# Scaling the second choice's rows on ScalarE and adding them on TensorE in the last turn from rows to columns

## The chip, the cores and the metric

The kernel runs on one core of one Trainium2 chip, as one program with one launch. The metric is the device time in microseconds (us) from start to end of an execution; smaller is better. Three runs of the kernel before gave a median of 8828.61 us (8826.25 to 8833.44).

## The reference

The model takes an image batch of 2 x 256 x 56 x 56 in f32 and applies four layers: a windowed attention, a positional embedding, six Mamba layers followed by a feed-forward over the better half of the tokens, and at last an attention over the two images and a mixture of 8 experts with two choices for each token. Only the end of the last layer is touched here:

```python
rw, re = jax.lax.top_k(probs, TOP_K)          # TOP_K = 2
rw = rw / jnp.maximum(rw.sum(-1, keepdims=True), 1e-12)
combine = jnp.zeros((N, E), tokens.dtype).at[jnp.arange(N)[:, None], re].set(rw)
out = tokens
for e in range(E):
    h = jax.nn.gelu(tokens @ w1[e] + b1[e], approximate=False)
    y = h @ w2[e] + b2[e]
    out = out + combine[:, e:e + 1] * y
...
x = _from_tokens(t, x)     # tokens x channels back to channels x tokens
```

So each token gets its own row plus two expert rows, each times a factor of its own, and the result is then turned from rows (a token in a partition) to columns (a channel in a partition) and written out.

## The kernel before

The span has three parts. The convolution part and the long Mamba part take it up to about 7900 us; neither is touched. The rest is the function `tail_phase`, in which the tokens lie as rows: each image (batch index `b`, 0 or 1) has 3136 tokens in 28 tiles of 112, and four tiles make a group, so that an image has seven groups, called g0 to g6 below.

The order of the instructions on every engine in that part is made by a small planner, the class `Flow` (L1199). Every piece of work is a Python generator. It yields `("take", name)` for a buffer of a ring, `need(flag)` for a condition, and an engine's name with a cost in us; the planner keeps one clock for each engine, resumes the generator that is due first, and what a generator issues at that moment is appended to the engines' queues. The costs thus decide the order, not the chip. On the chip each engine then runs its queue strictly in order and waits on semaphores. SP (SyncE) issues the plain DMAs, also strictly in order; POOL issues the gathers and scatters by index.

The mixture of experts runs in this order. Rows are gathered by expert (L1396, `pair<-m_d`), turned by TensorE into PSUM (L2005), copied by VectorE (L1340, `hid`), multiplied (L2030), copied back (L1340, `pair`), turned again (L2045), put through the Gelu by ScalarE (L2053, `deep`), multiplied again (L2030), copied by ScalarE (L1338, `out`) and scattered by POOL to a table `r2_d` in DRAM (L1986), whose first half holds every token's row from its first choice and whose second half that from its second choice. One such pass handles two blocks of 128 rows, and an image has 28 of them. PSUM tiles come from rings: three called `turn`, three called `mid`, two called `sum`.

`combine(b, g)` (L2069) closes a group. It adds the experts' biases to the tokens `t` (L2089), waits until all experts of that image are done, and then does for `c` = 0 and 1 (first and second choice): take one of the six buffers `rows`, load 112 x 4 x 256 values from `r2_d` into it (L2099, 448 KB), and add four tiles of it, each times its column of `gates`, to `t` by VectorE with `add_times` (L1388), after which the buffer is given back. Then `turn` transposes `t` group-wise into two `turn` tiles, one for each half of the 256 channels (L1348, four transposes to a tile), ScalarE copies both to a `chan` tile (L1338), and SP writes that to the output (L2114).

```python
def turn(dst, src, n, engines=("ACT", "DVE")):
    for k in range(2):
        ps = yield take("turn")
        for i in range(n):
            nc.tensor.transpose(ps[:, chunk(i, TK)], src(i)[:, chunk(k, P)], ident[:TK, :TK])
        yield "PE", 0.2 * n
        yield move(engines[k], dst[:, k, : n * TK], ps[:, : n * TK])
        flow.give("turn", ps)
```

The groups of image 0 are combined while the experts of image 1 run (about 8605 to 8750 us). The groups of image 1 come when no other work is left (8797 us to the end): fourteen loads, fifty-six adds, fifty-six transposes, fourteen copies, seven writes. In SP's queue the fourteen loads of image 1 stand one behind the other, first choices of g0 to g6, then second choices of g0 to g6, and the seven writes behind them. With six buffers, the first six loads start at once and the seventh to the fourteenth each wait for an add that gives a buffer back.

Of the kernel before, what the change touches and what calls it, by code (L numbers as in the profile page):

```python
# [15 lines left out]
AF = mybir.ActivationFunctionType  # L16
# [5 lines left out]
P = 128  # L22
# [23 lines left out]
TK = 112  # L46
# [4 lines left out]
GT = 4 * TK  # L51
# [8 lines left out]
def chunk(c, n=NT):  # L60
    return slice(c * n, (c + 1) * n)
# [1198 lines left out]
def tail_phase(ctx: ExitStack, tc: tile.TileContext, I, t2_d, out, rest):  # L1260
# [6 lines left out]
    nc = tc.nc  # L1267
# [7 lines left out]
    flow = Flow()  # L1275

    def fixed(shape, name, dtype=F32):
        return cp.tile(shape, dtype, name=name)
# [19 lines left out]
    def take(name):  # L1298
        return "take", name

    def need(*flag):
        return "need", flag

    ident = fixed([P, P], "tl_ident")
# [18 lines left out]
    t, mv, rs, up, off, score = [], [], [], [], [], []  # L1323
# [12 lines left out]
    def move(which, dst, src):  # L1336
        if which == "ACT":
            nc.scalar.copy(dst, src)  # L1338
        else:
            nc.vector.tensor_copy(dst, src)  # L1340
        return which, 0.65
# [10 lines that stand above are left out]
# [35 lines left out]
    def add_times(b, i, src, factor):  # L1387
        nc.vector.scalar_tensor_tensor(  # L1388
            t[b][:, i, :], src, factor, t[b][:, i, :], ALU.mult, ALU.add
        )  # L1390
# [105 lines left out]
    def per_batch(shape, name, dtype=F32):  # L1496
        return [fixed(shape, f"{name}_{b}", dtype) for b in range(B)]
# [4 lines left out]
    gates = per_batch([TK, 2, NTK], "gates")  # L1502
# [566 lines left out]
    def combine(b, g):  # L2069

        yield need("weighed", b)
        yield need("expert", b, 3 * g + 2)
        comb = yield take("comb")
        ps = yield take("mid")
        for n in range(4):
            nc.tensor.transpose(ps[:NE, chunk(n, TK)], lg[b][:, 4 * g + n, :], ident[:TK, :TK])
        yield "PE", 0.4
        yield move("ACT", comb, ps[:NE, :GT])
        flow.give("mid", ps)
        for n in range(0, 4, 2):  # L2080
            ps = yield take("mid")
            for i in range(2):
                nc.tensor.matmul(
                    ps[:TK, chunk(i, C)], lhsT=comb[:, chunk(n + i, TK)], rhs=mb2,
                    start=True, stop=True,
                )
            yield "PE", 0.9
            own = t[b][:, 4 * g + n : 4 * g + n + 2, :].rearrange("p n c -> p (n c)")
            nc.vector.tensor_tensor(own, own, ps[:TK], ALU.add)  # L2089
            yield "DVE", 0.7  # L2090
            flow.give("mid", ps)
        flow.give("comb", comb)
        for n in range(NQ // 2):
            yield need("expert", b, n)
        if b == 0:
            yield need("loaded_expert", 1, 3 * g + 1)
        for c in range(2):
            z = yield take("rows")
            nc.sync.dma_start(  # L2099
                z[:TK],  # L2100
                r2_d[b][c * S + g * GT : c * S + (g + 1) * GT, :].rearrange(
                    "(n p) c -> p n c", p=TK
                ),
            )
            yield "SP", 1.3
            yield "wait", 2.0
            for n in range(4):
                i = 4 * g + n
                add_times(b, i, z[:TK, n, :], gates[b][:, c, i : i + 1])
            yield "DVE", 2.0  # L2110
            flow.give("rows", z)
        o = yield take("chan")
        yield from turn(o, lambda i: t[b][:, 4 * g + i, :], 4, ("ACT", "ACT"))
        nc.sync.dma_start(out_v[b, :, :, chunk(g, GT)], o)  # L2114
        yield "wait", 3.0
        flow.give("chan", o)
# [54 lines left out]
    for b in range(B):  # L2171
        flow.start(*[back(b, g) for g in range(NG)])
        flow.start(*[combine(b, g) for g in range(NG)])
# [130 lines left out]
```

## Time and profile before

| what | value |
|---|---|
| runs: median (lowest to highest) | 8828.61 us (8826.25 to 8833.44) |
| profiled execution, its own time | 8834.56 us |
| its span, first to last instruction | 8832.8 us, mean granted TensorE clock 0.97 |
| PE / DVE / ACT / POOL busy over the span | 84% / 89% / 75% / 86% |
| a load of `rows` in the last stretch | 448 KB, 7.8 to 9.7 us from issue to landing |
| an add to `t` (L1388, 112x256) | 477 ns |
| a copy of a turned tile by ScalarE / by VectorE (128x448) | 532 ns / 615 ns |
| a transpose of 112x112 in the tail (L1348) | 257 ns at full clock, up to 450 ns |

Busy shares over the whole span are those of the Mamba part and say little about the tail; rows of single stretches have to be read. `busy` counts the time in which an engine works on an instruction; a DMA share near or above 1 means that all 16 DMA engines of the core are at work all the time. The granted clock is the share of full speed at which TensorE was let run. In the tail one column of the 40 slices is 221 us, so the last stretch of 35 us must be asked for by a window of its own.

### The profile page before, as it was taken

What the parts mean: (1) busy time and instruction counts of PE and PEld (TensorE: products, weight loads), DVE (VectorE), ACT (ScalarE), POOL (GpSimd) and SP (SyncE); (2) the same over time, 40 slices, a digit from 0 to 9 for tenths busy, and PEclk for the clock granted to TensorE, in tenths of its full rate; (3) what the DMA queues carried; (4) which work ended last, traced back from release to release, by engine and by line L of the source; (5) the groups of instructions that cost most, each with busy time, mean ns of one, the idle gap of its engine ahead of it and who ended that gap; (6) DMA issues with size and microseconds to landing.
All of it is one profiled execution on the core that took longest, in us unless ns stands there. A gap on an engine that the chain in (4) does not pass through costs nothing.

```text
span 8832.8 us, 106454 instructions
## 1 busy us (share of the span) xinstructions
PE 7458.7 (84%) x32350; PEld 3282.6 (37%) x32350; DVE 7845.9 (89%) x7140; ACT 6659.6 (75%) x15914; POOL 7609.8 (86%) x5255
## 2 busy tenths in 40 slices
PE   9988888888888888888888888888888888867987
PEld 6553333333333333333333333333333333325776
DVE  3339999999999999999999999999999999985664
ACT  1238888888888888888888888888888888863432
POOL 2339999999999999999999999999999999982354
PEclk9999999999999999999999999999999999988988
DMA  2335565655656555556566565556556565543225
GB/s 85 100 116 127 135 135 126 136 131 132 135 132 133 131 132 135 134 133 148 136 137 137 127 133 134 130 133 135 130 133 134 127 138 130 134 118 93 65 72 150
DMA packets 698246, 1118.31 MB, mean 127 GB/s; under 512 B 80060, under 2 KB 675843, under 8 KB 697667
## 3 DMA queue, kind: packets, MB, share of 16 engines
q1 hardware_dynamic: 682888, 1072.49, 52.5%
q0 software_dynamic: 14784, 39.01, 1.5%
q8 instruction: 257, 4.21, 0.2%
q14 instruction: 317, 2.60, 0.1%
HBM read 892.62 MB, written 218.60 MB: 126 GB/s over the span
## 4 chain that ended last, share of the span: by engine, by line
PE 44%; ACT 33%; DVE 13%; issue 6%; DMA 2%; POOL 2%; SPq 0%; ACTq 0%; DVEq 0%; POOLq 0%
ACT da L896 12%; PE mm L683 9%; PE mm L665 8%; PE mm L821 6%; DVE da L934 4%; PE acc L949 4%; DVE x L934 4%; ACT dt L742 2%; DVE x L926 2%; ACT dt L750 2%; ACT hz L695 2%; PE mm L754 2%; ACT dt L749 2%; ACT hz L700 2%; ACT dt L758 1%
## 5 line engine op out<-in xcount | busy, mean ns | idle before, releaser
L913 POOL TENSOR_TENSOR x<-dtur,bc 128x900 f32<-128x900 f32 x2688 | 4717.0, 1793 | 7.8 <-DMA dtur<-dtu_d 7.6
L896 ACT ACTIVATE da<-dtr,am 128x451 f32<-128x451 f32 x5376 | 3417.0, 641 | 323.7 <-DVE x L934 153.9
L934 DVE TENSOR_TENSOR_SCAN da<-da,x 128x902 f32<-128x902 f32 x1512 | 3040.1, 2031 | 97.5 <-ACT da L896 70.9
L934 DVE TENSOR_TENSOR_SCAN x<-da,x 128x902 f32<-128x902 f32 x1176 | 2341.5, 2018 | 46.6 <-ACT da L896 38.2
L926 POOL TENSOR_TENSOR x<-x,bc 128x896 f32<-128x896 f32 x1176 | 2080.1, 1784 | 80.9 <-DVE x L934 80.9
L926 DVE TENSOR_TENSOR x<-da,bc 128x896 f32<-128x896 f32 x1512 | 1604.1, 1075 | 20.5 <-ACT state L922 9.0
L949 PE MATMUL acc<-x,sum_w 128*32 128x448 f32 x10752 | 1382.5, 568 | 59.2 <-DVE x L926 33.9
L683 PE MATMUL mm<-u,w_cv 128*128 128x448 f32 x2656 | 1093.8, 554 | 67.0 <-ACT tail L678 56.9
L665 PE MATMUL mm<-xn,w_z 128*128 128x448 f32 x1328 | 587.0, 564 | 196.5 <-ACT dt L758 116.7
L683 PEld LDWEIGHTS mm<-u,w_cv 128*128 128x128 f32 x2656 | 478.6, 190 | 677.7 <-issue 375.9
L665 PE MATMUL mm<-xn,w_u 128*128 128x448 f32 x1328 | 579.0, 558 | 121.2 <-ACT hz L695 111.8
L821 PE MATMUL mm<-hz,w_out 128*128 128x448 f32 x1344 | 553.7, 555 | 107.9 <-ACT tail L678 56.3
L949 PEld LDWEIGHTS acc<-x,sum_w 128*32 128x32 f32 x10752 | 266.2, 111 | 966.7 <-issue 732.7
L754 PE MATMUL mm<-dt,mb_ident 128*128 128x448 f32 x666 | 342.1, 595 | 257.6 <-ACT state L922 139.4
L737 PE MATMUL mm<-xd,w_dt 128*128 128x448 f32 x664 | 339.2, 592 | 217.2 <-ACT dtu L745 128.6
L912 ACT COPY x<-state 128x2 f32<-128x2 f32 x2688 | 437.1, 187 | 0.1
L665 PEld LDWEIGHTS mm<-xn,w_z 128*128 128x128 f32 x1328 | 225.4, 189 | 564.5 <-ACT dt L758 236.4
L665 PEld LDWEIGHTS mm<-xn,w_u 128*128 128x128 f32 x1328 | 231.5, 189 | 457.8 <-ACT hz L695 223.1
L821 PEld LDWEIGHTS mm<-hz,w_out 128*128 128x128 f32 x1344 | 243.3, 191 | 417.9 <-issue 189.2
L766 POOL TENSOR_TENSOR dtu<-dt,hz 128x448 f32<-128x448 f32 x336 | 330.9, 985 | 76.6 <-PE mm L755 76.6
L695 ACT ACTIVATE hz<-mm,vec 128x448 f32<-128x448 f32 x332 | 209.2, 630 | 243.1 <-PE mm L683 238.8
L944 PE MATMUL acc<-hz,w_sk 128*128 128x448 f32 x672 | 347.0, 600 | 31.7 <-DVE hz L963 31.7
(377 smaller groups left out, 9536.9 us busy)
## 6 DMA issues: line engine op xcount, KB each, us to landing
dtr<-dt_d SPq DMA_DIRECT2D x1344, 224.0 KB, 4.4
dtur<-dtu_d SPq DMA_DIRECT2D x1344, 224.0 KB, 6.7
bc<-bc_d SPq DMA_DIRECT2D x336, 448.0 KB, 7.8
dt_d<-dt SPq DMA_DIRECT2D x336, 224.0 KB, 6.2
dtu_d<-dtu SPq DMA_DIRECT2D x336, 224.0 KB, 2.0
rows<-r_d SPq DMA_DIRECT2D x28, 448.0 KB, 7.9
xg<-in_x SPq DMA_DIRECT2D x26, 448.0 KB, 8.9
bm<-in_edge SPq DMA_DIRECT2D x16, 539.0 KB, 4.6
```

Of the source, the lines that this page charges most:

```text
L665: nc.tensor.matmul(ps, lhsT=w[:, k, chunk(d, P)], rhs=Q["xn"][:, k, :], start=(k == 0), stop=(k == 1),)
L683: nc.tensor.matmul(ps, lhsT=w_cv[:, 4 * d + k, :], rhs=M["u", d][:, k : k + T], start=(k == 0), stop=(k == 3),)
L695: nc.scalar.activation(hz(j)[:, d, :], M["mm"], AF.Identity, bias=layer_of(j + 1)["cb"][:, d : d + 1])
L754: nc.tensor.matmul(ps, lhsT=ident, rhs=M["dt"][:, d, :], start=True, stop=False)
L821: nc.tensor.matmul(ps, lhsT=layer_of(j - 1)["w_out"][:, d, chunk(k, P)], rhs=gated(j - 1)[:, d, :], start=(d == 0), stop=False,)
L896: nc.scalar.activation(D[i][:, chunk(g, R)], dtr[:, 2 * pr + g, :], AF.Exp, scale=L["am"][:, col : col + 1],)
L912: nc.scalar.copy(x[:, :, 0:1], states(i))
L913: nc.gpsimd.tensor_tensor(x[:, :, 1:], Q[k][1][:, 2 * pr : 2 * pr + 2, :], wide(Q["bc"][:, ng, :]), ALU.mult)
L926: engine.tensor_tensor(both(X[i])[:, :, 1 : T + 1], both(h)[:, :, 1 : T + 1], wide(QS[j]["bc"][:, 4 + ng, :T]), ALU.mult,)
L934: nc.vector.tensor_tensor_scan(h, D[i], X[i], 0.0, ALU.mult, ALU.add)
L944: nc.tensor.matmul(acc[0][:, :T], lhsT=L["w_sk"][:, k, :], rhs=Q["hz"][:, k, :], start=True, stop=False,)
L949: nc.tensor.matmul(acc[0][chunk(g, HD), :T], lhsT=sum_w, rhs=both(X[i - 1 + g // 2])[:, g % 2, 1 : T + 1], start=False, stop=(ng == 3), ti ...
```

## The change

For image 1 and the second choice (`b and c`), the four tiles of the loaded buffer are no longer added to `t` by VectorE: ScalarE multiplies each in place with its factor (an activation Copy with a scale from `gates`). The buffer is kept. Then the turn of image 1 is written out: for each half of the channels and each of the four tiles, two matmuls with the identity as the moving operand accumulate in the same PSUM place, one with the tile of `t` and one with the scaled tile as the stationary operand, in place of one transpose. The first half is copied to `chan` by VectorE, the second by ScalarE (both by ScalarE before). The buffer is given back only after both halves are turned and copied.

For image 0 the instructions stay the same, but the planner's cost of the four adds is 1.7 in place of 2.0, for image 1's first choices too.

```diff
             for n in range(4):
                 i = 4 * g + n
-                add_times(b, i, z[:TK, n, :], gates[b][:, c, i : i + 1])
-            yield "DVE", 2.0
+                factor = gates[b][:, c, i : i + 1]
+                if b and c:
+                    nc.scalar.activation(z[:TK, n, :], z[:TK, n, :], AF.Copy, scale=factor)
+                else:
+                    add_times(b, i, z[:TK, n, :], factor)
+            if b and c:
+                yield "ACT", 2.2
+            else:
+                yield "DVE", 1.7
+                flow.give("rows", z)
+        o = yield take("chan")
+        if b == 0:
+            yield from turn(o, lambda i: t[b][:, 4 * g + i, :], 4, ("ACT", "ACT"))
+        for k in range(2 * b):
+            ps = yield take("turn")
+            for n in range(4):
+                for x, last in ((t[b][:, 4 * g + n, :], False), (z[:TK, n, :], True)):
+                    nc.tensor.matmul(
+                        ps[:, chunk(n, TK)], lhsT=x[:, chunk(k, P)], rhs=ident[:TK, :TK],
+                        start=not last, stop=last,
+                    )
+            yield "PE", 1.6
+            yield move(("DVE", "ACT")[k], o[:, k, :], ps[:, :GT])
+            flow.give("turn", ps)
+        if b:
             flow.give("rows", z)
-        o = yield take("chan")
-        yield from turn(o, lambda i: t[b][:, 4 * g + i, :], 4, ("ACT", "ACT"))
         nc.sync.dma_start(out_v[b, :, :, chunk(g, GT)], o)
```

The planner's order on the engines for image 1 becomes: on ScalarE the 24 scalings of g0 to g5, then the copies of the second halves of g0 to g3, then the four scalings of g6, then the copies of g4 to g6; on SP the first thirteen loads, the write of g0, the fourteenth load (second choice of g6), then the writes of g1 to g6; on TensorE the turns of g0 to g3 interleaved, of which the second half of g3 needs a PSUM tile that ScalarE's copy of g0 frees. The fourteenth load goes into the buffer that held g0's second choice. For image 0 the order of SP shifts: before, its fourteen loads stand between the writes in runs of 4, 3, 1, 2, 3, 1; after, in runs of 4, 1, 1, 3, 1, 2, 2. The order of the expert passes' pieces among these shifts too.

## The prediction

> **What bounds the kernel now.** I read the page for the span first; its slices are 221 us wide, so the tail is asked for by windows, by the order of time in the last 45 us, and by the waits of the engines and of SP's queue. The page begins:
>
> ```profile
> span 8832.8 us, 106454 instructions
> ## 1 busy us (share of the span) xinstructions
> PE 7458.7 (84%) x32350; PEld 3282.6 (37%) x32350; DVE 7845.9 (89%) x7140; ACT 6659.6 (75%) x15914; POOL 7609.8 (86%) x5255
> ```
>
> These shares belong to the Mamba part, which the change doesn't touch. The order of time of the last stretch (start, length, engine, line, what, count, idle before):
>
> ```profile
> 8795.28 0.99 POOL L1986 DMA_INDIRECT r_d<-out,goal  x1 [0.30 <-issue]
> 8797.76 17.67 SPq L2099 DMA_DIRECT2D rows<-r_d  x14
> 8801.51 3.30 DVE L1388 SCALAR_TENSOR_TENSOR t<-rows,gates,t 112x256 f32<-112x256 f32 x8 [11.63 <-DMA rows<-r_d]
> 8805.09 19.85 DVE L1388 SCALAR_TENSOR_TENSOR t<-rows,gates,t 112x256 f32<-112x256 f32 x48 [0.28 <-DMA rows<-r_d]
> ...
> 8816.94 11.45 SPq L2114 DMA_DIRECT2D out<-chan  x7
> ...
> 8824.77 2.60 PE L1348 MATMUL turn<-tl_ident,t 112*128 112x112 f32 x16 [1.69 <-ACT chan L1338]
> 8826.35 1.64 ACT L1338 COPY chan<-turn 128x448 f32<-128x448 f32 x3 [0.34 <-DMA out<-chan]
> ```
>
> After the last scatter SP issues fourteen loads. VectorE adds from 8801.5 to 8824.9 almost without a break, which looks like a VectorE bound. The windows say that it is not alone (length; busy of PE, PEld, DVE, ACT, POOL; clock, DMA share, GB/s):
>
> ```profile
> 8808.00:8812.00 4.00, 0.00 (x0) 0.00 (x0) 4.00 (x10) 0.00 (x0) 0.00 (x0) 0.50 1.11 276
> 8814.00:8816.00 2.00, 2.00 (x8) 1.36 (x9) 2.00 (x6) 0.36 (x1) 0.00 (x0) 0.50 1.12 279
> 8820.00:8822.00 2.00, 2.00 (x10) 1.55 (x10) 2.00 (x6) 1.24 (x3) 0.00 (x0) 0.50 1.12 282
> 8822.00:8824.00 2.00, 1.07 (x9) 0.86 (x8) 2.00 (x6) 0.00 (x0) 0.00 (x0) 0.93 1.04 384
> 8826.00:8828.00 2.00, 1.37 (x8) 1.02 (x6) 0.00 (x0) 1.52 (x4) 0.00 (x0) 0.50 0.95 360
> 8828.00:8833.00 5.00, 0.00 (x0) 0.00 (x0) 0.00 (x0) 0.00 (x0) 0.00 (x0) 0.50 0.61 225
> ```
>
> The DMA engines are full from 8800 to 8828. Fourteen loads of 458,752 B at 279 GB/s are 23.0 us, seven writes at about 370 GB/s are 8.7 us: 31.7 us of the 35.0 from the first load's issue to the end. A group's four adds take 1.65 us (3.30 for two) and a load's transfer takes 1.64: two equal bounds side by side.
>
> Ahead of that, the experts of image 1 run beside image 0's combine (windows, then who waited for whom from 8600 to 8797, us in total, times, longest):
>
> ```profile
> 8610.00:8620.00 10.00, 3.97 (x19) 3.13 (x18) 2.96 (x6) 1.69 (x5) 7.86 (x8) 0.87 1.02 266
> 8640.00:8650.00 10.00, 6.13 (x30) 4.41 (x28) 3.87 (x8) 2.15 (x6) 7.78 (x8) 0.91 0.82 219
> 8710.00:8720.00 10.00, 7.49 (x30) 5.33 (x29) 3.67 (x8) 1.73 (x5) 7.87 (x8) 0.82 0.95 284
> ```
>
> ```profile
> PEld turn L2005 <- DMA pair<-m_d,pick: 23.3, 13, 5.4
> DVE t L1388 <- DMA rows<-r_d: 10.1, 5, 3.4
> SPq L2114 <- ACT chan L1338: 102.9, 6, 27.7
> ```
>
> TensorE is mostly busy there, and idles where a run of row loads fills the DMA engines and the experts' gathers land late. SP stands at a write for up to 27.7 us, and a load queued behind it stands too.
>
> **The change, part by part.** The sum is made against the profiled execution: span 8832.8, own time 8834.56, which is 5.95 us above the median of the runs; differences are carried over to the median.
>
> *VectorE, image 1.* 28 adds x 477 ns = 13.4 us go, seven copies x 615 ns = 4.3 us come. The seventh to thirteenth loads wait only for adds of first choices, which stay; so these loads start as now (8803.2 to 8813.4). As the DMA engines are full until 8822, the shorter VectorE work is worth nothing there. Of the 3.3 us between 31.7 and 35.0 the start of the first load and the end of the last write take most; what could be gained is about 1 us.
>
> *ScalarE, 28 scalings of 112x256.* The same form (Copy, scale by a column) of 128x128 at L636 took 389 ns, two in 0.68, so 0.29 apart; copies of 448 and 512 columns took 532 and 586 ns, 0.84 ns a column. 128 columns more make 497 ns, 0.40 apart: 1.69 us for a group of four. Below, L636 itself (four in 1.26); above, L1381 of the same width with one more operand (588 ns, four in 2.07). I take 1.69, the nearest form. The first scaling can start when the eighth load lands (issued 8804.8, landing 7.8 to 8.4 us later, 8812.6 to 8813.4); the thirteenth lands at 8820.3 to 8821.4. Six groups by ScalarE's pace end at 8822.3 to 8823.1, by the loads' pace at 8822.0 to 8823.1: I take 8822.8.
>
> *What is queued behind.* ScalarE runs in order, and the copy of g0's second half stands behind all 24 scalings; before it was done at about 8816.9. So the write of g0, which began at 8816.94, begins at 8822.8 + 0.53 + 0.1 = 8823.4. On SP the fourteenth load stands behind that write, and its buffer was g0's: before it was issued at 8815.12, now at 8823.4 + 0.4 = 8823.8, 8.7 us later. In between the DMA engines run dry: loads are through at 8821.
>
> *The end.* Landing of the fourteenth load: at most 3.75 us for the very first (issued 8797.76, its add began 8801.51, nothing ahead), 8.4 the median with the engines full. Now three writes are beside it and nothing is ahead but one: I take 5.0, nearer the empty end, so 8828.8. Four scalings: 1.69, to 8830.5. Then on TensorE the last pair (0.3), eight matmuls for g5 that stand in order ahead, and eight for g6's second half. A plain f32 matmul of 112 columns took 275 ns (L795) against 257 for a transpose, the pitch being that of weight loads: eight in 1.42 us at the half clock, sixteen transposes in 2.60 over mixed clock. Eight plain ones thus cost 0.86 to 1.6; I take 1.2 twice. A copy 0.53, and from the end of the last copy to the end of the span 4.84 as now (8827.99 to 8832.8). Sum: 8830.5 + 0.3 + 2.4 + 0.53 + 4.84 = 8838.6, 5.8 us more. Low end: scalings done 8822.3, landing 3.75, 0.86 twice, and a write that lands in 3.0 with 1.0 after it: 8835.2, +2.4. High end: ScalarE at 2.07 a group, landing 8.4, 1.6 twice: 8846, +13.2.
>
> *TensorE's other matmuls.* 112 in place of 56. The first 56 (to g2's second half) lie beside the scalings: 56 x 0.19 at half clock is 10.6 us from 8813.5 on, to 8824.1, which g0's write doesn't wait for. The cover is ScalarE's 9.7 us; if TensorE were slower by a half it would delay g2's and g3's writes, not the fourteenth load.
>
> The windows above show the clock at 0.50 from 8814 to 8822 although TensorE was busy in all that time with transposes, and 0.50 again at 8826 after a pause. The Trainium skill ("TensorE: Matmul & The Clock Gate", "What's actually happening") has the clock full after about 3.4 us of sustained work and halved after as long an idle window; in its Part 4 it says that transposes do not count as work. By the first rule this trace should have been at full speed from 8818, which it was not; with plain matmuls in their place the second would let the clock rise earlier. The last turns come after a wait of some us for the fourteenth load, and by the page they would run at half clock: the sum would be 0.8 us higher.
>
> *Image 0.* The instructions are the same and only the planner's order shifts. Two runs of three loads become shorter. Idle TensorE time in the windows of these runs was 6.0 (8610), 3.9 and 2.2 (8640, 8650), 2.9 (8680) and 2.5 us (8710), 17.5 in all; the first run stays. If half of the rest went, 5.8 us would be gained; as much could be lost where an expert's copy now stands behind an add that waits (10.1 us of such waits now). No row tells which, so the ends are -8 and +8; I take -1.
>
> Total: +5.8 - 1 = +4.8, on the median 8833.4.
>
> **The rivals.**
> 1. *The relief of VectorE counts* (the adds were the bound). For it: VectorE has no gap from 8805 to 8824.9. Against: the DMA share of 1.1. If the fourteenth load were not held, the end would come at most 1 us sooner: 8827.6 with image 0 at nothing.
> 2. *The smoother loads of image 0 outweigh the end.* For it: 11.5 us of idle time at the runs that change. Half gone and the low end of the tail: -5.8 + 2.4 = -3.4, 8825.2. To be below -0.2% it would need more than all of it.
> 3. *Slower beyond 0.2%: a load of image 0 caught behind a write in SP's queue.* In the new order loads stand singly behind writes, and an add in VectorE's queue that waits for such a load holds the experts' copies behind it. SP's longest wait of this kind is 27.7 us. It decides from 12 us of stall on (17.7 - 5.8). With 20 us: 8828.6 + 25.8 = 8854. Against it: the longest such wait of VectorE now is 3.4 us.
> That the change does not do what it says is excluded: the 28 activations and 112 matmuls are in the changed program.
>
> **How the numbers follow.** 0.2% of the median is 17.7 us, about what a measurement of this kernel can tell from no change. The held load with image 0 within its ends: 0.68 (own range 8826 to 8842). Rival 1: 0.06. Rival 2: 0.15. Rival 3: 0.08. Something large and faster that I do not see: 0.03. The first three stay within 0.2%: 0.89; slower 0.08; faster 0.03. The range of 8 in 10 takes the likeliest case with both unknown ends and most of rival 2: 8822 to 8846.
>
> **What would show it.** Right: ScalarE's scalings at about 0.40 us apart, done at 8822 to 8823; the fourteenth load issued some 8 us later than now; a hole in the DMA share before it; the last write issued about 6 us later after the last scatter. Wrong: scalings much slower than 0.5 us, the last scatter (8795.28 now) moved by more than 8 us, or no hole in the DMA share.

## The result

Over 20 runs each the kernel before has a median of 8834.83 us and the changed kernel one of 8849.74 us. The ratio is 1.0015, with a 95% interval of 1.0008 to 1.0021: 14.9 us slower by the medians, 7 to 19 us by the interval, nearly all of it inside the 0.2% that I had set as the bound of "no change". The predicted time of 8833.4 us was too low by 16.3 us, and the range (8822 to 8846) does not hold the measured time. Of these 16.3 us, 6.2 belong to the base: the three runs from which I started had a lower median (8828.61) than the twenty (8834.83). The other 10.1 us are a wrong size of the change itself, 4.8 predicted against 14.9.

The profiled execution of the changed kernel has a span of 8851.5 us. Every engine has the same instructions in the same order up to the scatter at 8537.7 us, the first after a pause of POOL. In this pair of profiles it came 8.5 us later (8546.2), and in a second profile of the changed kernel at 8536.2, so this is chance. So I compare two stretches by themselves: the experts' part, from that scatter to the last one (257.6 us before, 252.5 after; its 80 scatters are 24 of image 0 and the 56 of image 1, so that an expectation below errs where it has it begin with image 1), and the last stretch, from the issue of the first of the last fourteen loads to the end of the span (35.0 us before, 50.4 after). In this pair the whole loss is in the last stretch: 15.4 us longer, where I had predicted 5.8. Its order of time, in the changed kernel (start, length, engine, line, what, count, idle before):

```profile
8801.14 16.50 SPq L2099 DMA_DIRECT2D rows<-r_d  x13
8805.21 12.09 DVE L1388 SCALAR_TENSOR_TENSOR t<-rows,gates,t 112x256 f32<-112x256 f32 x28 [11.96 <-DMA rows<-r_d]
...
8817.35 6.64 ACT L2111 ACTIVATE rows<-rows,gates 112x256 f32<-112x256 f32 x16 [20.24 <-DVE t L1388]
...
8825.09 3.30 ACT L2111 ACTIVATE rows<-rows,gates 112x256 f32<-112x256 f32 x8 [1.10 <-issue]
...
8828.29 0.51 ACT L1338 COPY chan<-turn 128x448 f32<-128x448 f32 x1
...
8828.83 0.39 SPq L2135 DMA_DIRECT2D out<-chan  x1
...
8829.32 0.42 SPq L2099 DMA_DIRECT2D rows<-r_d  x1
```

The first write comes at 8828.83, 27.7 us after the first load's issue, and the fourteenth load 0.5 us behind it; that is the held load of the prediction. But it is not what ends last. The chain of waits of this stretch shows TensorE from its first scaled tile to the last copy:

```profile
8817.35 0.52 ACT rows L2111
8817.86 0.04 issue
8817.91 13.79 PE turn L2126 x94
8831.70 0.02 issue
8831.72 0.64 DVE chan L1340
8832.36 0.04 issue
8832.40 14.56 PE turn L2126 x128
```

And the windows (busy of PE, PEld, DVE, ACT, POOL; clock, DMA share, GB/s), first the whole stretch, then two cuts of it:

```profile
8801.10:8851.50 50.40, 29.09 (x224) 28.47 (x224) 16.08 (x35) 15.15 (x35) 0.00 (x0) 0.77 0.69 192
8820.00:8824.00 4.00, 4.00 (x20) 4.00 (x20) 0.62 (x1) 3.99 (x10) 0.00 (x0) 0.50 1.10 275
8824.00:8828.00 4.00, 4.00 (x37) 4.00 (x36) 0.62 (x1) 2.91 (x8) 0.00 (x0) 0.96 0.08 24
```

```profile
8797.80:8832.80 35.00, 11.62 (x56) 8.85 (x56) 23.09 (x56) 7.06 (x14) 0.00 (x0) 0.56 0.97 276
```

The last of these lines is the same stretch before. TensorE's records (a record is one instruction of the engine as the profile notes it) went from 56 to 224, four times as many for twice as many instructions of the program; its busy time went from 11.6 to 29.1 us, and the DMA engines, which had been full for the whole stretch (share 0.97), stood nearly idle at 8824 to 8828 (0.08). The two groups behind the 224 are:

```profile
L2126 PE MATMUL turn<-tl_ident,t x112: 275/275/555, 8805.8 to 8846.4; 112*128 112x112 f32 x112
L2126 PE MATMUL turn<-tl_ident,rows x112: 275/275/555, 8817.9 to 8846.7; 112*128 112x112 f32 x112
```

The program issues 56 matmuls on `t` and 56 on the scaled rows. Each one stands in the trace as two.

### The profile page after: what moved, and what is told of

Same layout as the page of the kernel before. It is cut to its first block, busy times and chain, and to the rows that moved or that the text cites. A ratio compares the mean times of both kernels' runs of the same rounds, so it can differ in the third digit from the quotient of the medians.

```text
span 8851.5 us, 106788 instructions
## 1 busy us (share of the span) xinstructions
PE 7502.3 (85%) x32518; PEld 3310.8 (37%) x32518; DVE 7839.4 (89%) x7119; ACT 6668.2 (75%) x15935; POOL 7609.2 (86%) x5255
## 4 chain that ended last, share of the span: by engine, by line
PE 45%; ACT 33%; DVE 13%; issue 5%; DMA 2%; POOL 1%; SPq 0%; ACTq 0%; DVEq 0%; POOLq 0%
ACT da L896 12%; PE mm L683 9%; PE mm L665 8%; PE mm L821 6%; DVE da L934 4%; PE acc L949 4%; DVE x L934 4%; ACT dt L742 2%; DVE x L926 2%; PE mm L754 2%; ACT dt L750 2%; ACT hz L695 2%; ACT dt L749 2%; ACT hz L700 2%; ACT dt L758 1%
```

## The experiments

Two theories. **A**: TensorE bounds the stretch, since a plain f32 matmul stands in the trace as two records, each with its own weight load, where a transpose stands as one. **B**: my prediction's own reason, the fourteenth load held behind the write of g0 and that behind ScalarE's scalings, was the right one and only came out larger. All runs below but one are single profiles; the last stretch is compared, since the part ahead of it wanders by more than the question. The speed of the row loads differs from run to run and must be kept in mind: in the ten us from the sixth us of the stretch on, it was 278 GB/s in the first profile of the kernel before, 266 in the first of the changed one, and between 236 and 290 in the others.

**The changed kernel again.**

> The changed kernel once more, as a measure of how far two profiles of one kernel differ: the last stretch 50.4 us within 1 us, image 0's combine (first scatter of the experts to last scatter, 252.5 us in the first profile) within 3 us if the 5 us that it gained on the kernel before are real, and more apart if they are chance.

The last stretch took 48.4 us (loads at 281 GB/s), the experts' part 255.8 us. So one kernel's last stretch moves by 2 us, twice what I expected. Of these, 1.3 us lie in TensorE's first 94 records (12.50 us in place of 13.79, as the clock rose earlier) and 0.8 in their start, 16.0 in place of 16.8 us after the first load's issue. The experts' part was 3.3 us longer than in the first profile, so that the 5 us of its gain were already down to 2.

**One transpose in place of two matmuls.**

```diff
-                for x, last in ((t[b][:, 4 * g + n, :], False), (z[:TK, n, :], True)):
-                    nc.tensor.matmul(
-                        ps[:, chunk(n, TK)], lhsT=x[:, chunk(k, P)], rhs=ident[:TK, :TK],
-                        start=not last, stop=last,
-                    )
+                nc.tensor.transpose(
+                    ps[:, chunk(n, TK)], z[:TK, n, chunk(k, P)], ident[:TK, :TK]
+                )
```

> The changed kernel with each pair of plain matmuls replaced by one transpose of the scaled tile; the tile of t is left out of the output of image 1, so that part of the sum is not computed. Scalings, buffers, copies and queue orders stay. Measured is the last stretch, from the issue of the first of the last fourteen loads to the end of the span (35.0 us before, 50.4 after). Theory A (TensorE: 224 records at 0.112 us in place of 56 bound the stretch): TensorE falls to 56 records, and what is left is the held fourteenth load, so 41 us (38 to 45), with TensorE idle for most of the stretch. Theory B (the fourteenth load held behind the write of g0 carries the whole loss): 47 to 50 us, since that load is still held.

The last stretch fell to 40.0 us, from 48.4 in the changed kernel on the same chip: theory A's number, and far from B's. Its window, its ScalarE and its SP show what is left:

```profile
8793.40:8833.40 40.00, 14.07 (x56) 9.90 (x56) 16.01 (x35) 14.95 (x35) 0.00 (x0) 0.50 0.85 242
```

```profile
8809.25 9.97 ACT L2111 ACTIVATE rows<-rows,gates 112x256 f32<-112x256 f32 x24 [19.91 <-DVE t L1388]
8819.12 1.36 ACT L1338 COPY chan<-turn 128x448 f32<-128x448 f32 x3
8820.73 0.53 ACT L1338 COPY chan<-turn 128x448 f32<-128x448 f32 x1 [0.24 <-PE turn L2125]
8824.73 1.71 ACT L2111 ACTIVATE rows<-rows,gates 112x256 f32<-112x256 f32 x4 [3.47 <-DMA rows<-r_d]
```

```profile
8793.37 16.13 SPq L2099 DMA_DIRECT2D rows<-r_d  x13
8819.66 0.40 SPq L2133 DMA_DIRECT2D out<-chan  x1
8820.14 0.42 SPq L2099 DMA_DIRECT2D rows<-r_d  x1
```

This is the stretch that I had predicted for the changed kernel, almost to the step: 24 scalings in 9.97 us (9.7 predicted), the fourteenth load issued 26.8 us after the first (26.0 predicted), its scalings begun 4.6 us later (5.0), the end at 40.0 us (40.8). The chain that I worked out exists. It lies hidden under TensorE's in the changed kernel.

**A buffer of its own for the fourteenth load.**

```diff
-            z = yield take("rows")
+            alone = b and c and g == NG - 1
+            if alone:
+                z = h0[g]
+            else:
+                z = yield take("rows")
...
-        if b:
+        if b and not alone:
             flow.give("rows", z)
```

> The changed kernel with a buffer of its own for the fourteenth load (second choice of g6), so that SP issues all fourteen loads ahead of the first write. TensorE's 224 records stay. Last stretch: Theory A (TensorE bounds): the load comes early but TensorE is busy without a break, so 48 to 50.4 us, at most 2 us less. Theory B (held load): 42 to 44 us, 6 to 8 us less.

50.9 us, against 48.4 and 50.4 for the changed kernel (loads at 254 GB/s against 281 and 266). SP issued all loads ahead of the first write: the one into the buffer of its own (`h0[g]`, a tile of an earlier phase) 15.3 us after the first, where the changed kernel issued it 26 to 28 us after. Nothing came of it:

```profile
8797.37 15.26 SPq L2103 DMA_DIRECT2D rows<-r_d  x12
8812.67 0.53 SPq L2103 DMA_DIRECT2D h<-r_d  x1
8814.12 1.01 SPq L2103 DMA_DIRECT2D rows<-r_d  x1
8827.55 17.18 SPq L2139 DMA_DIRECT2D out<-chan  x7
```

```profile
8814.83 13.67 PE turn L2130 x94
8828.51 0.02 issue
8828.53 0.64 DVE chan L1340
8829.17 0.04 issue
8829.21 14.56 PE turn L2130 x128
```

TensorE's two runs are as long as in the changed kernel, 13.67 and 14.56 us against 13.79 and 14.56. Theory B is out: a load that comes over 10 us earlier is worth nothing while TensorE has 28 us of work in a row.

**Both edits.**

> Both edits together: one transpose of the scaled tile in place of each pair of matmuls (t of image 1 left out of the output) and a buffer of its own for the fourteenth load. Last stretch: Theory A with the held load as the second bound: 36 to 39 us. What then is left over the 35.0 us of before is the wait of ScalarE's copies behind its scalings. Theory B: 36 to 39 us as well; if neither is the whole of it, it stays above 41 us.

38.7 us, in the range of both theories. With TensorE's work down, the early load is worth 1.3 us of 40.0, with the loads of this run at 290 GB/s against 278. That is less than the 2 to 5 us that I had expected between these two; it is a single pair of runs, and the copies still stand behind the scalings on ScalarE.

**All copies by VectorE as well.**

```diff
-            yield move(("DVE", "ACT")[k], o[:, k, :], ps[:, :GT])
+            yield move("DVE", o[:, k, :], ps[:, :GT])
```

> One transpose of the scaled tile (t of image 1 left out of the output), a buffer of its own for the fourteenth load, and all copies of turned tiles by VectorE, so that no copy stands behind a scaling on ScalarE. Last stretch: 34 to 36 us if held load, TensorE and the copies behind the scalings are all that the change costs; the DMA share should show no hole before the writes. If it stays above 37 us, another cost is in it.

38.4 us, above the number that I gave; but this run had its loads at 259 GB/s, and the kernel of the next experiment, whose end is that of the kernel before, took 37.0 us on the same chip at the same rate of loads. Against that it is 1.4 us longer. The DMA share had no hole any more (0.83 and above in every 2 us from 8840 to 8852). I had given an absolute time where only a difference could hold; on this chip there is no large further cost.

**The planner's cost alone.**

```diff
-            yield "DVE", 2.0
+            yield "DVE", 2.0 if b and c else 1.7
```

> The kernel before with the planner's cost of four adds at 1.7 in place of 2.0 (2.0 kept for image 1's second choices): the order of image 0's combine and of the experts of image 1 is that of the changed kernel, the end is that of the kernel before. Last stretch: 35.0 us within 1 us. If the new order is worth what the two first profiles show (257.6 us before, 252.5 after, from the first scatter to the last), the kernel is 3 to 7 us faster than before (ratio 0.9992 to 0.9997); if that is chance, the same within 2 us; if the order loses and only the profile hid it, 3 us slower or more.

The ratio to the kernel before is 0.9996, with a 95% interval of 0.9987 to 1.0005, from 11 runs against 15 (8860.7 and 8863.15 us on a chip on which both run slower than on the first). The last stretch took 37.0 us, 2.0 more than I expected, with VectorE 23.3 us busy as in the kernel before and TensorE 13.3 (11.6 there); its loads ran at 259 GB/s against 278. So the new order of image 0 and of the experts costs at most 4.4 us and gains at most 11.5: a gain of 3 to 7 us is neither shown nor excluded. The profiles lean towards the gain without showing it: in the experts' part the old order took 257.6, 262.8, 253.2 and 267.7 us in four profiles (mean 260.3), the new one 252.5, 255.8, 248.4, 255.2, 254.2, 255.2, 258.3, 257.9 and 261.7 in nine (mean 255.5). They overlap, and they come from different chips.

**Plain matmuls in the kernel before.**

```diff
-        yield from turn(o, lambda i: t[b][:, 4 * g + i, :], 4, ("ACT", "ACT"))
+        if b == 0:
+            yield from turn(o, lambda i: t[b][:, 4 * g + i, :], 4, ("ACT", "ACT"))
+        for k in range(2 * b):
+            ps = yield take("turn")
+            for n in range(4):
+                nc.tensor.matmul(
+                    ps[:, chunk(n, TK)], lhsT=t[b][:, 4 * g + n, chunk(k, P)],
+                    rhs=ident[:TK, :TK], start=True, stop=True,
+                )
+            yield "PE", 0.8
+            yield move("ACT", o[:, k, :], ps[:, :GT])
+            flow.give("turn", ps)
```

> The kernel before with the transposes of image 1's turn replaced by plain matmuls with the identity, one for each tile (no scaling by ScalarE, no second matmul). Theory A: TensorE shows 112 records for these 56 matmuls, two for each, and 0.22 us for a matmul at full clock; the stretch is paced by adds and loads, and only the last 16 matmuls come out: 35.0 + 1 to 3 us. If a plain matmul cost what a transpose does: 56 records and 35.0 us within 0.5.

```profile
L2118 PE MATMUL turn<-tl_ident,t x112: 275/275/556, 8845.2 to 8860.9; 112*128 112x112 f32 x112
```

112 records for 56 matmuls, without a scaling or a sum in PSUM anywhere near. The last stretch is 39.7 us, above the 36 to 38 that I gave and 2.7 more than the 37.0 of the planner's cost alone on the same chip; but its loads were slower too (236 against 259 GB/s), so how much of the 2.7 is TensorE's stays open. The count is what this run was for.

**One plain matmul in the changed kernel.**

```diff
-                for x, last in ((t[b][:, 4 * g + n, :], False), (z[:TK, n, :], True)):
+                for x in (z[:TK, n, :],):
...
-                        start=not last, stop=last,
+                        start=True, stop=True,
```

> The changed kernel with the scaled tile's matmul alone (the tile of t is left out of image 1's output): 56 plain matmuls and so 112 records on TensorE, with everything else as in the changed kernel. If the loss is TensorE's time, it lies between the 40.0 us of the one transpose and the 50.4 and 48.4 us of the two matmuls: the TensorE work after the fourteenth load's scaling halves, so 41 to 44 us. If a chain of two matmuls into one PSUM place costs by itself (not by the count of records), it is 40 us.

43.1 us, in the range given, with 112 records and 18.8 us of TensorE, on another chip, with the loads at 256 GB/s:

```profile
8792.10:8835.20 43.10, 18.79 (x112) 17.94 (x112) 16.05 (x35) 15.21 (x35) 0.00 (x0) 0.62 0.82 224
```

With half the records TensorE no longer works without a break: the chain that ends last runs through the held fourteenth load, as in the run with one transpose, and then through TensorE's last twelve instructions. Here is this end, first with transposes, then with plain matmuls:

```profile
8825.29 3.15 PE turn L2125 x12
```

```profile
8825.22 5.42 PE turn L2126 x24
```

Of the 3.1 us between the two runs, 2.3 lie here, in twice the records; 1.2 lie in a fourteenth load that was issued later (28.0 against 26.7 us after the first, with slower loads), and 0.4 come back at the end. In a row: 56 transposes 40.0 us, 56 plain matmuls 43.1, 112 plain matmuls 48.4 and 50.4. A chain of two matmuls into one PSUM place isn't needed for the loss: a record begins 0.112 us after the one before at full clock, with such a chain (the changed kernel) and without it (this run).

**Two transposes, added by VectorE.**

```diff
+            own = yield take("mid")
-            for n in range(4):
-                for x, last in ((t[b][:, 4 * g + n, :], False), (z[:TK, n, :], True)):
-                    nc.tensor.matmul(
-                        ps[:, chunk(n, TK)], lhsT=x[:, chunk(k, P)], rhs=ident[:TK, :TK],
-                        start=not last, stop=last,
-                    )
-            yield "PE", 1.6
-            yield move(("DVE", "ACT")[k], o[:, k, :], ps[:, :GT])
+            for to, x in ((ps, t[b][:, 4 * g : 4 * g + 4, :]), (own, z[:TK])):
+                for n in range(4):
+                    nc.tensor.transpose(
+                        to[:, chunk(n, TK)], x[:, n, chunk(k, P)], ident[:TK, :TK]
+                    )
+            yield "PE", 1.2
+            yield move("ACT", o[:, k, :], ps[:, :GT])
             flow.give("turn", ps)
+            nc.vector.tensor_tensor(o[:, k, :], o[:, k, :], own[:, :GT], ALU.add)
+            yield "DVE", 0.7
+            flow.give("mid", own)
```

> The changed kernel with the two matmuls of a tile replaced by two transposes, one of t and one of the scaled tile, into two PSUM tiles; ScalarE copies the first to the output tile and VectorE adds the second to it. All is computed. TensorE has 112 records in place of 224. Theory A: TensorE no longer bounds, the held load does: last stretch 41 to 45 us (the adds of VectorE lie beside it). Theory B: 47 to 50 us.

44.0 us, with 112 records. This computes all that the changed kernel does, 4 to 6 us quicker in the last stretch (on another chip), and is still 7.0 us longer than the kernel with the old end on the same chip.

**The kernel before again, and without its second adds.**

> The kernel before once more, for the spread of its last stretch and of image 0's combine: the last stretch 35.0 us within 1 us on a chip like the first, up to 37 on one whose loads are slower; from the first scatter of image 1's experts to the last 257.6 us within 4 us on a chip like the first.

> The kernel before without the four adds of the second choice for image 1 (one add of a single column reads the loaded buffer in their place, so that buffers, loads and turns wait as before; the second choice of image 1 is left out of the output). VectorE has 28 adds of 0.48 us less, which is 13.4 us. If the loads fill the DMA engines and bound the stretch beside VectorE, it is at most 1 to 2 us shorter than the kernel before on the same chip. If VectorE was the bound, 6 us or more.

These two ran on one chip. The kernel before took 38.1 us, longer than I allowed, with the loads at 245 GB/s (and its experts' part 262.8 us, 5.2 over the first profile where I allowed 4); without the 28 adds it took 38.2, at 244 GB/s:

```profile
8805.10:8843.20 38.10, 12.52 (x56) 9.31 (x56) 23.33 (x56) 7.26 (x14) 0.00 (x0) 0.59 0.96 253
```

```profile
8796.20:8834.40 38.20, 13.60 (x56) 10.06 (x56) 12.79 (x35) 7.26 (x14) 0.00 (x0) 0.50 0.97 253
```

The first line is the kernel before, the second the one without second adds. VectorE's busy time falls from 23.3 to 12.8 us and the stretch stays as it is; the DMA share is 0.96 and 0.97. To take work from VectorE here is worth nothing, whatever it costs elsewhere.

No version that computes the whole output had a shorter last stretch than the kernel with the old end. Only the planner's cost alone was run often enough to compare whole times, and it came out level.

## Why the prediction was wrong, point by point

*What bounds the last stretch before.* Right. The full DMA engines carry it, and 10.5 us less of VectorE are worth 0 within the spread of the loads.

*ScalarE.* Right in size: 497 ns for a scaling against 493 measured, 0.40 us apart against 0.41. Its last scaling of g5 ended 27.3 us after the first load's issue where I had 25.0: the loads of that run were slower (266 GB/s against 278), the first scaling began 0.6 us later than my latest time for it, and ScalarE stood for 1.1 us before the last eight of the 24.

*The held load.* Right as a mechanism and in size, as the run with one transpose shows (40.0 us against 40.8). Wrong as the reason for the loss: the kernel with a free buffer lost as much. The chain that I summed was the second longest. My signs could not tell the two apart: the scalings' pace and the hole in the DMA share came as forecast, the fourteenth load was issued 10.8 us later where I had some 8, and no sign of being wrong appeared. Only the last write, 16 us later after the last scatter in place of 6, gave the miss away.

*TensorE.* This is the step that failed. I wrote that eight plain matmuls cost 0.86 to 1.6 us, "112 in place of 56", and that the first 56 lie beside the scalings. I took a record's duration (275 ns against 257) and the pitch of one weight load (the time from one record's start to the next) for a whole matmul, and did not compare the count of records with the count of instructions. Eight plain matmuls are sixteen records, 1.8 us at full clock and 3.4 at half, and the first 56 ended some 6 us after the scalings that were to cover them. The rows had it. In the same tail `combine` issues two bias matmuls for each add, and the trace before has

```profile
L2083 PE MATMUL mid<-mb,comb x72: 374/374/764, 8547.8 to 8768.2; 8*112 8x256 f32 x72
```

beside eighteen adds (L2089): 36 matmuls, 72 records. A plain f32 matmul is two records; a transpose (56 in the program, 56 in the row) is one. With 0.112 us for a record at full clock (128 records in 14.56 us) the 112 matmuls are 25 us, not 12, and at half clock they cost 0.213 a record. TensorE's first scaled tile is there 16.8 us after the first load's issue. From there on it is 13.79 + 14.56 us plus 0.70 between, then a copy and the last write: 16.8 + 29.1 + 0.6 + 4.0, ending 50.4 us after that issue. A sum that multiplied by two would have found 25 us of TensorE against 9.7 us of cover and put TensorE first.

The Trainium skill has a word on this that I passed over. "TensorE: Matmul & The Clock Gate", in its table of terms, calls the transpose mode four times faster for FP32, and "FP8 and Floating Point Precision", in "TensorE Precision Notes", gives true FP32 four passes. These runs show a factor of two in records, and of 2.3 in time at full clock: a plain matmul takes 2 x 0.112 us, a transpose 0.096 (four in 0.38 us in the run with two transposes). How many passes stand behind a record they don't show. Either figure of the pages would have been enough to put TensorE on the path.

*The clock.* I had weighed that plain matmuls would bring the clock up earlier than transposes, and they did: it rose from 0.50 to 1.00 at 8824.3, 6.4 us after TensorE began to work without a break, and after 3.7 to 6.3 us in the four other runs with plain matmuls at the end. That transposes never bring it up, as I took it, does not hold: in the kernel before they did so alone, after 8 us (0.50 until 8822, 0.93 in the next 2 us), and in the run with two transposes 4.3 us into a row of them. But the row of 24 transposes in 6.7 us of the run with one transpose did not, nor the 40 in 10.3 us of the planner's cost alone; both stayed at 0.50 for the whole stretch. What decides between these was not tested. The clock softened the loss: at half clock throughout, by 0.213 us a record, I estimate 27.5 us for the last 128 records, not 14.6.

*Image 0.* I took -1 with ends of -8 and +8. The run of the planner's cost alone gives a ratio of 0.9996 (0.9987 to 1.0005), which fits, and does not tell the sign. The last stretch is 13 to 15 us longer (48.4 and 50.4 against 35.0, at similar rates of the loads); with the experts' part, the two profiles of the changed kernel are 10 and 12 us longer than the first of the kernel before, against the 14.9 of the medians (7 to 19 by the interval). Against its second profile, on a chip with slower loads, it is only 2 and 3 us. So single profiles do not add up to the medians, and what is left over stays open.

*The rivals.* Rival 1 (the relief of VectorE) is excluded by the run without second adds, rival 3 (a load of image 0 caught) by the run of the planner's cost alone, which has image 0's new order (its loads stand on SP in the same runs of 4, 1, 1, 3, 1, 2, 2) and is not slower by more than 0.05%; rival 2 stays unsettled in its gain but was outweighed. That TensorE becomes the bound was not among them.

*The range.* It ended at 8846 because its high end came from the same missing term, and because it was laid around the median of three runs, 6.2 us lower than the twenty later showed. Moved up by that it would end at 8852 and hold the measured 8849.7, though the change itself was three times the forecast; it is the last stretch that shows the wrong step.

## What to carry to other kernels

Before an instruction is costed by the duration of its nearest row, count that row's records against the instructions that the program issues for it: a plain f32 matmul is two, a transpose one, so that "add it while turning" costs four records for one. A wait that one finds is not yet the path; sum every engine's own work from the moment at which its first input can be there, and let the sum that ends last win. And where the DMA engines are full, as they were here, taking work off a busy engine gained nothing, while the engine that took it over became the bound.

## What the runs showed of the hardware

- A plain f32 matmul of 112x112 with the identity shows as two records of 275 ns each, 0.112 us apart at full clock, with a weight load of 192 ns each; a transpose of the same tile as one record of 257 ns, 0.096 us apart, with a weight load of 141 (at half clock 0.213 and 0.187 us apart).
- After idle time TensorE's clock went from 0.50 to 1.00 after 3.7 to 6.4 us of plain matmuls, in all five runs that had them in the last stretch. With transposes it went up after 8 us in the first profile of the kernel before (8814 to 8822) and 4.3 us into a row of them in the run with two transposes, and not at all in the run with one transpose (24 in 6.7 us) and in that of the planner's cost alone (40 in 10.3 us).
- The same row loads ran at 236 to 290 GB/s in different runs, and the last stretch of one kernel took 35.0 us at 278 GB/s and 38.1 at 245; fourteen loads at these rates are 23.1 and 26.2 us.
